# One state in eight with TensorE's product of dt*u and B, and background pieces, norms and tanh placed at other steps

## The chip, the cores and the metric

The kernel runs on one core of a Trainium2 chip. The core has five engines that work side by side and take their instructions in order: TensorE (PE, matrix products, with its weight loads PEld), VectorE (DVE), ScalarE (ACT), GpSimd (POOL) and SyncE (SP, which here issues most DMA transfers). Arrays lie in SBUF, 128 partitions wide; TensorE writes into PSUM, which has eight banks of 128 x 512 floats. The metric is the device time of one execution in microseconds (us).

## The reference

Sixteen sequences of 512 positions and 256 features pass through two layers, each with a residual and a layer norm. The first is a selective state-space model (forward, then a second one over its convolved output, backward), 512 channels wide with 16 states a channel; the second is a soft mixture of 16 experts with 64 slots each. Cut to what matters:

```python
xf, res = jnp.split(x @ in_proj_w.T, [D_INNER], axis=-1)
xf = silu(causal_dw_conv(xf, conv_w, conv_b))
y  = ssm(xf, res, ...)                        # forward
xb = silu(causal_dw_conv(xf, conv_b_w, conv_b_b))
y  = y + ssm(xb, res, ..., reverse=True)
x  = layernorm(x + y @ out_proj_w.T)
x  = layernorm(x + moe(x))                    # moe: see below

# in ssm: delta, B, C are projections of u (u = xf or xb)
dt = softplus(delta @ dt_proj_w.T + dt_proj_b)
dA   = einsum('bld,dn->bldn', dt, A)
dB_u = einsum('bld,bld,bln->bldn', dt, u, B)
dA_cum = exp(suffix_sum(dA))
xs = cumsum(dB_u * dA_cum, 1) / (dA_cum + 1e-12)
y  = einsum('bldn,bln->bld', xs, C) + u * D
y  = y * silu(res)

# in moe: x and the slot embeddings are normed
logits   = einsum('bnd,esd->bnes', x, se)
dispatch = softmax(logits, axis=1)            # over positions
combine  = softmax(logits over all slots)
slots = einsum('bnd,bnes->besd', x, dispatch)
eout  = (gelu(slots @ Wg + bg) * (slots @ Wu + bu)) @ Wd + bd
out   = einsum('bns,bso->bno', combine, eout)
```

All of it is in 32-bit floats.

## The kernel before

A tile has 128 channels as its partitions and the 512 positions along the free dimension; a direction has four such tiles (c = 0 to 3). The scan of a batch is four parts: forward and backward of tiles 0 and 1, then forward and backward of tiles 2 and 3 (`scan_part(b, r, p, ...)`, r the direction, p the pair of tiles). A part goes over the 16 states in eight pairs (n = 0, 2, ... 14) and the two tiles: 16 units a part, 64 a batch, 1,024 in all. A unit does, for two states of one tile:

- POOL, L356: `db = du * bs`, 128 x 1024, with du = dt*u of the tile (L304) and bs the two rows of B, spread over all partitions by a DMA (L352);
- ScalarE, for each state: `h = exp(A*dt)` into a PSUM bank of a ring of three (L361), and `th = tanh(...)` into SBUF (L363), which is the factor that the 1e-12 of the reference leaves;
- VectorE, for each state: the recurrence as one scan instruction, in place in PSUM (L365 forward, L367 backward), then `hg = (th + 1) * h` (L370);
- POOL, L371: `hg = hg * cs`, 128 x 1024, with cs the two rows of C;
- TensorE, L320: eight transposing products that add hg into an accumulator in PSUM (`add_up`, two units later).

db has three buffers, hg four, cs two, bs three.

Everything else is cut into pieces that are laid beside the units. A piece is what a generator does between two yields. `yield k` says that the next piece takes k PSUM banks of a ring of three (`bank`); `yield HOLD` says that TensorE's result is to be taken up at the next step. Three queues of the class `Side` hold the generators: `prep` (convolutions, projections, dt and rr of the parts to come; one piece at every unit), `front` (`finish`: output projection, norm and the dispatch of the batch before) and `back` (`experts` for two batches, then `combine` for each of the two). `front` and `back` are paced: a credit grows by the steps still to do over the units still to come, and a credit of one lets one piece go. `beside_scan` runs after every unit: it first takes up what is held in each queue, then lets each lay its piece. A queue that has just taken up a result may lay its next piece in the same step. A piece that takes banks goes only where the ring has room:

```python
oldest = min([x.hold for x in sides if x.hold is not None], default=count[0])
if count[0] - oldest + self.need > BANKS:
    break
```

At the end of a batch `front` is emptied, and `back` after every second batch. The tail, after the scan, has eight banks for the pieces: it empties what is left, with the last `finish`, and then does the last two batches' experts and combines.

Names that the change and the steps of the prediction touch: `scan_part` (L341) and its instructions above; `prep_pair` (L263), which makes dt, rr and du; `project_unit` (L240), which writes the rows of B and C to DRAM (bc); `Side.go`, `take_up`, `piece` (L391 to L422); `finish` (L503) with the norm (L533 to L549); `dispatch` (L567) with pl, et, pd, pq; `experts` (L627) with pg, pu, peo; `weights` (L761) with cl, cm, ctp; `combine` (L811) with cpo, its loads of the experts' results (ceo) and its norm (L857 to L860, scaled at L497). In `combine` a column of ones beside the experts' results gives the softmax's sum as column 257 of cpo, and VectorE inverts it (L853).

A scheduler orders the instructions of each engine; where the code says `late`, an instruction keeps its place in the program's order.

## Time and profile before

| | us |
|---|---|
| median of 3 runs | 5471.18 (5466.05 to 5471.56) |
| the profiled execution | 5474.83 |
| its span, first to last instruction | 5473.0 |
| db (L356), 1,024 instructions on POOL | 2424.6 |
| hg*cs (L371), 1,024 instructions on POOL | 2422.2 |
| scans (L365 and L367), 2,048 on VectorE | 2447.8 |
| (th+1)*h (L370), 2,048 on VectorE | 1349.1 |
| exp and tanh (L361, L363), 4,096 on ScalarE | 2854.7 |
| transposing products (L320), 8,192 on TensorE | 1219.4 |

The profile names an instruction by its line, engine, operation and tile. "Busy" is the time in which an engine executed; "idle before" is the time that it stood before instructions of a group, with what ended it. TensorE's clock is granted by a throttle; the profile gives the granted share. The scan ends some 278 us before the span does. The prediction shows the lines that it rests on.

### The profile page before, as it was taken

How to read it: one execution, taken by the hardware profiler on the slowest of the kernel's cores; microseconds unless marked ns; L12 is line 12 of the kernel's file. 1: busy time of each engine (PE TensorE's matmuls, PEld its weight loads, DVE VectorE, ACT ScalarE, POOL GpSimd, SP SyncE). 2: the span in 40 equal slices, each digit the busy share in tenths (PEclk: the TensorE clock that was granted, in tenths of full speed). 3: DMA queues.
4: the chain of work that ended last, by engine and by line, in shares of the span. 5: the costliest groups of instructions: out<-in, count | busy, mean ns of one | idle time of the engine just before them, and what ended most of it. 6: DMA issues, size and time to landing. Idle time of an engine off the chain costs nothing.

```text
span 5473.0 us, 67758 instructions
## 1 busy us (share of the span) xinstructions
PE 4001.2 (73%) x21317; PEld 3106.7 (57%) x21330; DVE 4522.5 (83%) x6212; ACT 4101.0 (75%) x6665; POOL 5003.5 (91%) x2547
## 2 busy tenths in 40 slices
PE   4556656677787777777777777877777776778887
PEld 2434444565555665566556655555655665567656
DVE  6787878889898888888888898989888888888722
ACT  6667777778778777878777887787778787778641
POOL 6999999999999999999999999999999999989700
PEclk7567777888998998889899888988988898999999
DMA  4333333465546664366544655455544666457435
GB/s 131 112 112 123 122 118 121 157 206 186 166 137 193 198 191 150 131 205 208 177 138 157 204 186 170 136 193 193 192 149 136 200 203 189 139 168 250 135 104 174
DMA packets 493949, 897.77 MB, mean 164 GB/s; under 512 B 44403, under 2 KB 291827, under 8 KB 493589
## 3 DMA queue, kind: packets, MB, share of 16 engines
q1 hardware_dynamic: 454836, 851.48, 48.4%
q10 hardware_dynamic: 38752, 41.95, 2.2%
q8 instruction: 169, 2.77, 0.2%
q14 instruction: 192, 1.56, 0.1%
HBM read 832.47 MB, written 60.82 MB: 163 GB/s over the span
## 4 chain that ended last, share of the span: by engine, by line
DVE 33%; ACT 24%; PE 19%; issue 11%; POOL 10%; DMA 3%; SPq 0%; DVEq 0%; ACTq 0%; POOLq 0%
DVE h L367 9%; DVE h L365 8%; DVE hg L370 8%; ACT h L361 5%; ACT th L363 5%; POOL db L356 4%; POOL hg L371 4%; PE acc L320 3%; PE px L247 2%; PE pg L718 2%; DVE rr L302 2%; PE cl L770 2%; ACT L361 2%; PE peo L703 2%; ACT ht L740 1%
## 5 line engine op out<-in xcount | busy, mean ns | idle before, releaser
L356 POOL TENSOR_TENSOR db<-du,bs 128x1024 f32<-128x1024 f32 x1024 | 2424.6, 2368 | 118.9 <-DVE h L365 50.5
L371 POOL TENSOR_TENSOR hg<-hg,cs 128x1024 f32<-128x1024 f32 x1024 | 2422.2, 2365 | 26.2 <-DVE hg L370 17.6
L370 DVE SCALAR_TENSOR_TENSOR hg<-th,h 128x512 f32<-128x512 f32 x2048 | 1349.1, 678 | 253.4 <-ACT th L363 139.7
L320 PE MATMUL acc<-ident,hg 128*128 128x128 f32 x8192 | 1219.4, 302 | 383.9 <-POOL hg L371 312.9
L320 PEld LDWEIGHTS acc<-ident,hg 128*128 128x128 f32 x8192 | 1074.4, 158 | 622.3 <-POOL hg L371 402.3
L367 DVE TENSOR_TENSOR_SCAN h<-h,db 128x512 f32<-128x512 f32 x1024 | 1226.2, 1219 | 191.5 <-ACT h L361 148.3
L365 DVE TENSOR_TENSOR_SCAN h<-h,db 128x512 f32<-128x512 f32 x1024 | 1221.6, 1219 | 181.9 <-ACT h L361 134.1
L361 ACT ACTIVATE h<-dt,A_f 128x512 f32<-128x512 f32 x1024 | 700.0, 684 | 316.6 <-DVE hg L370 313.8
L361 ACT ACTIVATE h<-dt,A_b 128x512 f32<-128x512 f32 x1024 | 699.8, 683 | 297.6 <-DVE hg L370 296.1
L363 ACT ACTIVATE th<-rr,Ah_b 128x512 f32<-128x512 f32 x1024 | 728.0, 711 | 0.3
L363 ACT ACTIVATE th<-rr,Ah_f 128x512 f32<-128x512 f32 x1024 | 726.9, 710 | 0.2
L703 PE MATMUL peo<-Wd,ht 128*128 128x256 f32 x1024 | 321.0, 469 | 196.2 <-DVE ht L687 136.0
L703 PEld LDWEIGHTS peo<-Wd,ht 128*128 128x128 f32 x1024 | 227.4, 232 | 269.7 <-DVE ht L687 143.0
L718 PE MATMUL pg<-st,Wg 128*128 128x128 f32 x2048 | 280.1, 300 | 77.4 <-ACT xb L222 39.7
L770 PE MATMUL cl<-seT,cx 128*128 128x512 f32 x512 | 275.7, 681 | 74.0 <-DVE rr L302 35.7
L718 PEld LDWEIGHTS pg<-st,Wg 128*128 128x128 f32 x2048 | 270.5, 215 | 87.5 <-ACT xb L222 41.2
L675 PE MATMUL pu<-st,Wu 128*128 128x128 f32 x2048 | 268.7, 287 | 30.4 <-ACT ht L740 11.8
L675 PEld LDWEIGHTS pu<-st,Wu 128*128 128x128 f32 x2048 | 256.5, 202 | 52.5 <-ACT ht L740 13.2
L574 PE MATMUL pl<-x2T,seT 128*128 128x512 f32 x512 | 260.0, 632 | 24.3 <-DVE xf L171 14.6
L606 PE MATMUL pq<-dis,xn 128*128 128x256 f32 x1024 | 254.6, 406 | 15.4 <-ACT dis L596 12.7
L844 PE MATMUL cpo<-ceo,ct 128*128 128x257 f32 x1024 | 244.1, 393 | 25.5 <-ACT ct L799 16.4
L606 PEld LDWEIGHTS pq<-dis,xn 128*128 128x128 f32 x1024 | 206.3, 207 | 49.8 <-ACT dis L596 15.6
(147 smaller groups left out, 5149.9 us busy)
## 6 DMA issues: line engine op xcount, KB each, us to landing
bs<-bc SPq DMA_DIRECT2D x512, 512.0 KB, 4.6
cs<-bc SPq DMA_DIRECT2D x512, 512.0 KB, 3.7
Wg<-in_Wg_dram SPq DMA_DIRECT2D x128, 512.0 KB, 5.4
Wu<-in_Wu_dram SPq DMA_DIRECT2D x128, 512.0 KB, 5.8
Wd<-in_Wd_dram SPq DMA_DIRECT2D x128, 512.0 KB, 5.9
bd<-in_bd_dram SPq DMA_DIRECT2D x128, 128.0 KB, 4.7
s_dram<-sl ACTq DMA_DIRECT2D x64, 256.0 KB, 3.0
st<-s_dram SPq DMA_DIRECT2D x128, 128.0 KB, 4.5
```

The source lines that it names most:

```text
L320: ins = nc.tensor.matmul(accs[c][:, s], hc[:, j, s], ident, is_transpose=True, start=False, stop=(last and j == 1 and lc == NL - 1),)
L356: nc.gpsimd.tensor_tensor(db, du.unsqueeze(1).to_broadcast([P, 2, L]), bs, ALU.mult)
L361: nc.scalar.activation(h, dt, AF.Exp, scale=w["A"][:, c, s])
L363: nc.scalar.activation(th, rr, AF.Tanh, bias=LN_1E12 / 2, scale=w["Ah"][:, c, s])
L365: nc.vector.tensor_tensor_scan(h, h, db[:, j, :], 0.0, ALU.mult, ALU.add)
L367: nc.vector.tensor_tensor_scan(h[:, ::-1], h[:, ::-1], db[:, j, ::-1], 0.0, ALU.mult, ALU.add)
L370: nc.vector.scalar_tensor_tensor(hg[:, j, :], th, 1.0, h, ALU.add, ALU.mult)
L371: nc.gpsimd.tensor_tensor(hg, hg, cs, ALU.mult)
L606: nc.tensor.matmul(pq[:, k * 256 : (k + 1) * 256], xn[:, lc, k * P : (k + 1) * P], dis[:, lc, :], start=(lc == 0), stop=(lc == NL - 1),)
L675: nc.tensor.matmul(pu[:, fc * P : (fc + 1) * P], got["Wu", e][:, k, fc * P : (fc + 1) * P], st[:, k, :, j * SL : (j + 1) * SL], start=(k = ...
L703: nc.tensor.matmul(po[:, :DM], ht[:, fc, :], got["Wd", e][:, fc, :], start=(fc == 0), stop=(fc == NF - 1))
L718: nc.tensor.matmul(pg[:, fc * P : (fc + 1) * P], got["Wg", e][:, k, fc * P : (fc + 1) * P], st[:, k, :, j * SL : (j + 1) * SL], start=(k = ...
```

## The change

1. States 5 and 13 of the 16 (`DIAG`) no longer get their product dt*u*B from POOL. In the pairs n = 4 and 12, POOL's db and the load bs have one state (k = 1). For the other, TensorE multiplies the transposed du (duT) by a diagonal matrix of B's row, 128 positions at a time, into a PSUM bank of the pieces' ring (`by_diagonal`), one unit ahead. The decay exp(A*dt) of that state goes to SBUF (dec), and VectorE scans with dec and the bank. The diagonals lie in DRAM, zeroed once; `project_unit` writes B's rows into them as single floats with a stride of 129, by a DMA of ScalarE's queue, and SP loads each as a 128 x 512 tile (dg) one pair of states ahead. duT is made at the start of each part (`turn_pair`: eight transposes, two copies by ScalarE).
2. A yield of GAP + k marks a piece that needs what was just taken up: it isn't laid in the step in which its queue took something up (except in the last batch, `hurry`). A yield of WAIT ends the queue's work for this step. Norms are scaled two such steps after their statistics.
3. tanh is issued one state ahead of exp; th has four buffers.
4. `combine` sums the softmax by ScalarE's accumulator at the exp, instead of a column of ones; et, yt, sl and others share one tag of two buffers (fr), and the experts' results the ring of weights (W). `back` is no longer emptied after every second batch.

The diff, cut to its core:

```diff
+DIAG = (5, 13)
+DIAG_SIZE = P * (P + 1)
...
-HOLD = -1
+HOLD, WAIT, GAP = -1, -2, 8
...
                 late(nc.scalar.activation(xf, xf, AF.Silu))
+                yield WAIT
                 yield from project_unit(b, 0, out)
...
             nc.sync.dma_start(bc[1], xd[XC:XW, :])
+            step = DIAG[1] - DIAG[0]
+            nc.scalar.dma_start(
+                diag_dram[r].rearrange("i l (p s) -> i l p s", p=P)[:, :, :, 0],
+                xd[XB + DIAG[0] : XB + NS : step, :].rearrange("i (l p) -> i l p", p=P),
+            )
...
+        def turn_pair(b, r, p, v):
+            yield 2
+            pts = []
+            for c in (2 * p, 2 * p + 1):
+                pt = bank(f"pdu_{b}_{r}_{c}")
+                for lc in range(NL):
+                    s = slice(lc * P, (lc + 1) * P)
+                    nc.tensor.transpose(pt[:, s], v[c][2][:, s], ident)
+                pts.append((c, pt))
+            yield HOLD
+            for c, pt in pts:
+                duT = p4.tile([P, L], F32, tag="duT", name=f"duT_{b}_{r}_{c}", bufs=2)
+                late(nc.scalar.copy(duT, pt))
+                v[c].append(duT)
...
             prep.drain()
-            prep.gens += [[1, g] for g in then]
+            prep.gens += [[1, g] for g in [turn_pair(b, r, p, v)] + then]
+            def by_diagonal(n, c):
+                diags.append(count[0])
+                made[n, c] = h = bank(f"hd_{b}_{r}_{n}_{c}")
+                for lc in range(NL):
+                    s = slice(lc * P, (lc + 1) * P)
+                    ins = nc.tensor.matmul(h[:, s], v[c][3][:, s], dg[:, s], start=True, stop=True)
...
+            gates = [tanh(*units.pop(0))]
             for n in range(0, NS, 2):
+                k = 1 if n + 1 in DIAG else 2
...
+                if n + 3 in DIAG:
+                    dg = p4.tile([P, L], F32, tag="dg", name=f"dg_{q}", bufs=1)
+                    nc.sync.dma_start(
+                        dg.rearrange("p (l s) -> p l s", l=NL),
+                        diag_dram[r, DIAG.index(n + 3), :, : P * P].rearrange("l (p s) -> p l s", p=P),
+                    )
...
-                    nc.gpsimd.tensor_tensor(db, du.unsqueeze(1).to_broadcast([P, 2, L]), bs, ALU.mult)
+                    nc.gpsimd.tensor_tensor(
+                        db[:, :k, :], du.unsqueeze(1).to_broadcast([P, k, L]), bs[:, :k, :], ALU.mult
+                    )
...
+                        if j < k:
+                            dec = h = ps_h.tile([P, L], F32, tag="h", name=f"h_{q}_{c}_{j}")
+                            hs[j] = (h, dec, db[:, j, :])
+                        else:
+                            h = made.pop((n + j, c))
+                            dec = p4.tile([P, L], F32, tag="dec", name=f"dec_{q}_{c}", bufs=2)
+                            hs[j] = (h, dec, h)
+                    for j in range(2) if k == 2 else (1, 0):
+                        nc.scalar.activation(hs[j][1], dt, AF.Exp, scale=w["A"][:, c, n + j : n + j + 1])
+                        if units:
+                            gates.append(tanh(*units.pop(0)))
...
-                            nc.vector.tensor_tensor_scan(h, h, db[:, j, :], 0.0, ALU.mult, ALU.add)
+                            nc.vector.tensor_tensor_scan(h, dec, add, 0.0, ALU.mult, ALU.add)
...
+                    nxt_n = n if c == chunks[0] else n + 2
+                    if nxt_n + 1 in DIAG:
+                        for x in sides:
+                            x.take_up()
+                        by_diagonal(nxt_n + 1, chunks[1] if c == chunks[0] else chunks[0])
                     beside_scan()
+                    if k == 1:
+                        diags.pop(0)
                     add_up(2)
...
             def take_up(self):
-                if self.hold is not None:
+                self.took = self.hold is not None or self.wait
+                if self.took:
                     self.go()
...
-                while self.gens and self.hold is None:
-                    oldest = min([x.hold for x in sides if x.hold is not None], default=count[0])
+                while self.gens and self.hold is None and not self.wait:
+                    if self.gap and self.took and gaps:
+                        break
+                    oldest = min([x.hold for x in sides if x.hold is not None] + diags[:1], default=count[0])
...
-            yield 0
+            yield WAIT
+            yield WAIT
             scaled(xt, xt, sh, rs)
...
-                yield 1
+                yield GAP + 1
                 pt = bank(f"pd_{i}")
...
-            for cm, cl in zip(cms, cls):
-                nc.scalar.activation(cm, cl, AF.Exp, bias=nm[:, 2:3])
-            yield 2
+            sm = p3.tile([P, 3], F32, tag="csm", name=f"csm_{i}", bufs=2 * NL)
+            for h, (cm, cl) in enumerate(zip(cms, cls)):
+                nc.scalar.activation(cm, cl, AF.Exp, bias=nm[:, 2:3], accum_out=sm[:, h : h + 1])
+            yield GAP + 2
...
             if kept is None:
                 stats = norm(0, NL)
-                yield 0
+                yield WAIT
+                yield WAIT
                 put(0, NL, *stats)
...
             front.drain()
-            if b % 2 == 0:
-                back.drain()
```

## The prediction

> **What bounds the kernel now.** First the busy shares and the slices of the page:
>
> ```profile
> PE 4001.2 (73%) x21317; PEld 3106.7 (57%) x21330; DVE 4522.5 (83%) x6212; ACT 4101.0 (75%) x6665; POOL 5003.5 (91%) x2547
> ...
> POOL 6999999999999999999999999999999999989700
> ```
>
> POOL is full until the scan ends and has nothing to do in the last two slices, so the run is a scan that POOL seems to pace (48 to 5195 us; L881 closes a batch, and its times give 323 us for batch 0, 317 to 324 for 1 to 14, 343 for 15) and a tail. Second, busy time by stage (columns: length, then PE, PEld, DVE, ACT, POOL busy, granted clock, DMA share, GB/s): batch 0, the heavy batches 3 to 14, roughly the last batch, and the two parts of the tail.
>
> ```profile
> 48.00:371.00 323.00, 165.11 (x724) 126.50 (x726) 267.17 (x310) 216.95 (x328) 319.10 (x151) 0.61 0.34 117
> 960.00:4800.00 3840.00, 2902.69 (x15862) 2267.55 (x15875) 3361.42 (x4603) 3055.08 (x4965) 3738.98 (x1878) 0.89 0.54 175
> 4800.00:5195.00 395.00, 320.97 (x1894) 263.43 (x1893) 323.65 (x483) 297.73 (x505) 347.83 (x174) 0.94 0.59 186
> 5195.00:5289.00 94.00, 76.37 (x285) 48.84 (x283) 20.93 (x51) 38.06 (x72) 4.96 (x12) 0.93 0.27 87
> 5289.00:5473.00 184.00, 148.78 (x861) 126.25 (x860) 42.20 (x128) 43.64 (x103) 9.71 (x32) 0.93 0.56 168
> ```
>
> Batch 0 carries little beside the scan (TensorE 51% busy), a heavy batch much (76%), and both take some 320 us: POOL is the bound in both, 319 of 323 us and 3739/12 = 311.6 of 320. But in a heavy batch VectorE is at 3361/12 = 280.1 us, and what it waits for comes third (waits of DVE, 960 to 4800 us):
>
> ```profile
> DVE h L365 <- ACT h L361: 117.3, 76, 4.8
> DVE hg L370 <- ACT th L363: 101.9, 51, 5.6
> DVE h L367 <- ACT h L361: 93.8, 79, 4.6
> DVE hg L370 <- PE acc L320: 35.2, 46, 2.1
> ```
>
> These and the smaller entries are about 427 us, 35.6 a batch, nearly all on ScalarE. With 4.3 us of gaps too small to be listed VectorE's own loop fills its 320 us. POOL's queue has been hiding that; take POOL's work away and VectorE is next. Fourth, where ScalarE comes late (timeline):
>
> ```profile
> 2169.70 0.69 ACT L361 ACTIVATE h<-dt,A_f 128x512 f32<-128x512 f32 x1 [1.85 <-DVE hg L370]
> ...
> 2175.74 2.08 ACT L497 ACTIVATE cx<-cx,c_sh,c_rs 128x256 f32<-128x256 f32 x4 [5.35 <-POOL c_sh L492]
> 2177.72 0.71 ACT L363 ACTIVATE th<-rr,Ah_f 128x512 f32<-128x512 f32 x1
> ...
> 2178.46 0.69 DVE L370 SCALAR_TENSOR_TENSOR hg<-th,h 128x512 f32<-128x512 f32 x1 [5.30 <-ACT th L363]
> ```
>
> The norm's scaling waits 5.35 us for statistics that stand behind two full-size products in POOL's queue; the tanh behind it is late, and VectorE stands for 5.30 us.
>
> **The change, part by part.** Prices, as total busy and mean ns:
>
> ```profile
> L356 POOL TENSOR_TENSOR db<-du,bs 128x1024 f32<-128x1024 f32 x1024 | 2424.6, 2368 | 118.9 <-DVE h L365 50.5
> L304 POOL TENSOR_TENSOR du<-dt,xf 128x512 f32<-128x512 f32 x64 | 80.0, 1272 | 9.7 <-ACT dt L285 9.5 <-ACT dt L289 0.2
> L333 PE MATMUL acc<-diagD_f,xf 128*128 128x128 f32 x512 | 77.8, 302 | 0.0
> L512 PE MATMUL pyt<-ident,res 128*128 128x128 f32 x256 | 40.3, 281 | 0.0
> ```
>
> *Removed.* Two states of sixteen lose their POOL product: 16 batches x 4 parts x 2 pairs x 2 tiles = 256 of 1,024 db shrink from 1024 to 512 columns. A 512-column product is 1.27 us (L304), so 2.37 - 1.27 = 1.09 us each, 279 us in all, 17.4 a batch. Exact halving would give 303; I take the row. The column of ones, its memsets (14 x 0.125 us) and 64 reciprocals go; sums, 128 accumulator reads (0.19 us each, as at L585) and small operations on VectorE come: under 2 us a batch.
>
> *Added on TensorE.* 1,024 products with a diagonal. L333 in both directions is 512 such products in the program, 1,024 instructions and 149 us here, so two instructions of 0.1455 us each: 298 us, 1.16 per unit. Turning du: 512 transposes at 40.3/256 = 0.157, 81 us. Together 379 us, 23.7 a batch; a heavy batch goes from 242 to some 261 of TensorE after what leaves for the tail (below). What hides it is TensorE's free quarter, at about 85% of 310 us no wide cover: the last stage of the scan ran at 81% and its batch took 343 us.
>
> *Added on ScalarE.* Eight copies a batch at 0.577 us (L517) = 4.6 us, accumulator reads 1.5; the 256 decays written to SBUF cost 27 ns more each (711 against 684, th and h). It had 255 of 320 us; 261 remain under 310. The first copy of du is due four units into a part; before it the part's pieces only wait.
>
> *Waits.* VectorE's second scan of a unit now waits for TensorE's product. Behind that wait stand the unit's second h*(th+1), then POOL's hg, then the next transposes. The product is issued one unit earlier, right behind the transposes of the unit four back; these end about when db of its own unit does, and the other state's 1.9 us (1.22 + 0.68) go first on VectorE. No row shows this wait: its ends are 0 and, were TensorE to begin only when VectorE asks, transposes (8 x 0.149) and product, 2.35 us x 16 = 38 us a batch. I take 2 us a batch: nearest is the 35.2 us in 12 batches that VectorE waits for acc, 2.9 a batch. Other end, a gain: these decays need no h buffer, 1/8 of the 211 us of waits on exp, 2.2 a batch. I let the two cancel.
>
> *Moved.* Norms two steps behind: in 1602 to 2244 us four such stalls (4.29, 3.40, 5.30, 1.85) cost VectorE 14.8 us in two batches, 7.4 a batch, gone if POOL answers within two units (9 us; it took 5 to 6.5). Tanh one ahead: the other tanh waits are (101.9 - 82)/12 < 2 a batch; I count 1. TensorE's pieces a step behind: TensorE waited 120 + 116 + 114 us on et, ht and cm in the heavy stage; that is TensorE's cover, worth nothing by itself.
>
> *DMA.* SP's queue gets 128 loads of a 256 KB diagonal, and the bs of 128 steps shrinks by 256 KB: bytes equal. The load stands ahead of cs and is issued units before its use; a load like it landed in 4.5 us (st). ScalarE's queue gets 32 writes of 1,024 single floats; a column load of 512 floats (D_f, 2 KB) landed in 2.3 us, so some 5 us, at least four units (18 us) ahead of the read. Without that cover: 32 x 5 = 160 us.
>
> The Trainium skill, "DMA: Bandwidth & Descriptors" (Latency and other measured facts), speaks against such writes: below 512 bytes a transfer is done by read-modify-write, off line rate. No row shows that price; by the rule they land later than my 5 us, which changes the sum only once the 18 us are used up, and then by up to the 160 us named.
>
> *The tail.* A piece that needs a copy just taken up now starts a step later, and the product holds one or two of the three PSUM banks in 6 of 16 steps. Followed through the queues, the background falls behind: when the scan ends, before leaves 5 of 13 steps of one combine; after leaves 10 of 40 expert steps and two whole combines. In instructions behind the last acc that is 64 pg, 80 pu, 40 peo, 48 cl, 48 ctp and 96 cpo more; at the tail's own busy time per instruction (0.128, 0.124, 0.274, 0.456, 0.154, 0.231) 80.6 us. The first part of the tail had 94 - 76.4 = 17.6 us of TensorE idle, which can hide some 10: +70.
>
> *The sum.* Batches 0 to 2, bound by POOL: 3 x 17.4 = -52. Heavy: POOL would allow 320 - 17.4 = 302.6; VectorE's loop 320 - 7.4 - 1 - 3 (waits that POOL's side caused) + 1 = 309.6. The later decides: 10.4 x 12 = -125. Batch 15 has fewer background steps (44 for 61): -12. Tail +70. Total -119. The profiled execution was 5474.8 us (5473.0 span), 0.07% over the median of 5471.2: 5471 - 119 = 5352, say 5355.
>
> **Rivals.** (a) *POOL stays the bound everywhere*: -279, -5 more as batch 15 has fewer background steps, +67 for the tail: 5471 - 217 = 5254. For it: light and heavy batches take the same time, so VectorE's waits looked free. Against: only 10 of 320 us separate its loop from POOL. Chance 0.17. (b) *The bound passes to VectorE and ScalarE at once*, as their waits do not shrink: heavy batches 316 to 320: 5430 to 5476. For it: 211 of 427 us are waits on exp, which the change hardly touches. Chance 0.16, 0.05 of it within 0.2%. (c) *Slower: TensorE's product comes late.* TensorE at 85% with in-order waits and one or two banks fewer; every unit of the two states holds VectorE for the product's own 1.16 us. Then 309.6 + 16 x 1.16 = 328 a heavy batch, 12 x 18.6 = +223: 5578. It decides from (5482 - 5355)/(12 x 16) = 0.66 us a unit. For it: the 343 us batch; against: a unit of lead. Chance 0.21. That the change does not do what it says is small: in its program 256 db have 512 columns.
>
> **How the numbers follow.** Forecast 0.46, around 5355 (5300 to 5420). Faster 0.46 + 0.17 + 0.11 = 0.74, within 0.2% 0.05, slower 0.21; 0.2% is what a measurement of this kernel can tell. The range, 5240 to 5510, takes in (a), (b) and the near half of (c).
>
> **What would show it.** Right: db x256 at 1.27 us and POOL near 4,720 us; no wait of cx or x on sh in the scan; heavy batches of 306 to 313 us; a tail of 348 us after the last L881 for 278. Wrong: waits of DVE on hd over 0.7 us a unit; POOL idle over 25 us a heavy batch; TensorE without the 379 us; a tail that did not grow.

## The result, and the profile after

The changed kernel takes 5470.31 us (median of 12 runs, 5459.48 to 5473.61), the kernel before, on the same chip, 5469.6 us (12 runs, 5460.49 to 5473.56): ratio 1.000 (95% interval 0.9991 to 1.0009). No change can be told. The profiled execution spans 5468.7 us, 4.3 us less than before's 5473.0.

Behind the zero stand moves of tens of microseconds. A batch ends with VectorE's last product of res and acc (L881 before, L987 after); by the times at which these start:

| stage | before, us | after, us | change | predicted |
|---|---|---|---|---|
| batches 0 to 2 (to the end of batch 2) | 1006.98 | 950.25 | -57 | -52 |
| heavy batches 3 to 14 | 3844.8 | 3870.5 | +26 | -125 |
| batch 15 | 343.3 | 317.1 | -26 | -12 |
| tail, behind the last such line | 277.9 | 330.9 | +53 | +70 |
| span | 5473.0 | 5468.7 | -4 | -119 |

The light batches, the last one and the tail went roughly where the prediction put them. The heavy ones did not: 323.2 us each (mean of 4 to 14) for 320.4 before and 309.6 predicted. First the page of the kernel after: busy time with its share of the span and the count, and POOL in 40 slices.

```profile
PE 4239.6 (78%) x23889; PEld 3381.1 (62%) x23890; DVE 4512.5 (83%) x6275; ACT 4164.7 (76%) x6906; POOL 4733.4 (87%) x2537
...
POOL 6999999999989989998998989999999989998400
```

POOL has lost 270 us, as meant (5003.5 before), and its row of nines has gaps: it now waits. Busy time by stage of the kernel after (length, then PE, PEld, DVE, ACT, POOL busy, granted clock, DMA share, GB/s): batch 0, batches 4 to 14, batch 15, and the two parts of the tail.

```profile
48.00:355.00 307.00, 179.12 (x882) 139.14 (x884) 262.30 (x305) 224.82 (x342) 299.90 (x150) 0.70 0.39 126
1266.00:4821.00 3555.00, 2824.44 (x16184) 2260.44 (x16185) 3083.60 (x4268) 2850.49 (x4715) 3248.96 (x1714) 0.90 0.54 171
4821.00:5138.00 317.00, 263.01 (x1597) 218.34 (x1595) 263.26 (x380) 246.92 (x421) 277.34 (x146) 0.90 0.59 186
5138.00:5232.00 94.00, 84.18 (x428) 63.27 (x428) 26.77 (x76) 35.40 (x79) 3.28 (x8) 1.00 0.58 179
5232.00:5469.00 237.00, 206.66 (x1092) 163.32 (x1092) 62.01 (x184) 72.48 (x175) 13.11 (x40) 0.97 0.47 144
```

In batch 0 POOL is busy 300 of 307 us: there it still paces, and the batch ends 12.5 us sooner (batches 1 and 2 are 22 us shorter each). In a heavy batch it is busy 3249/11 = 295.4 of 323.2 us and idles 28: it has stopped being the bound, and the batch did not get shorter. No engine is full there: VectorE 280.3, TensorE 256.8, ScalarE 259.1. So the time is in what they wait for. Waits of VectorE, 960 to 4800 us, in the kernel after (total, times, longest):

```profile
DVE h L442 <- ACT h L433: 187.4, 89, 9.9
DVE h L440 <- ACT h L433: 69.9, 43, 5.5
DVE ht L784 <- PE pu L772: 60.3, 25, 9.1
DVE hd L442 <- PE hd L388: 34.8, 25, 3.9
DVE xf L182 <- ACT xf L176: 28.7, 11, 5.0
DVE hg L445 <- PE acc L354: 26.5, 26, 4.6
```

The 101.9 us of waits on tanh (hg <- th) are gone from the head of the list, but the waits on exp have grown from 211 to 257 us, and new ones on TensorE have come: pu, the product hd, and xf. One of the stalls on exp, in the timeline of ScalarE in the kernel after (start, us, what):

```profile
3229.57 1.28 ACT L240 ACT_TABLE_LOAD   x1
3230.86 1.92 ACT L240 ACTIVATE xb<-xb 128x2048 f32<-128x2048 f32 x1
3232.69 0.56 ACT L612 COPY yt<-pyt 128x512 f32<-128x512 f32 x1
3233.27 1.28 ACT L834 ACT_TABLE_LOAD   x1
3234.56 0.37 ACT L834 ACTIVATE ht<-pg,bg_cols 128x128 f32<-128x128 f32 x1
3234.83 1.91 ACT L837 ACTIVATE ht<-pg,bg_cols 128x128 f32<-128x128 f32 x7
3236.75 1.28 ACT L433 ACT_TABLE_LOAD   x1
3238.04 0.69 ACT L433 ACTIVATE h<-dt,A_f 128x512 f32<-128x512 f32 x1
```

and in VectorE's (in brackets the idle time before it and who ended it):

```profile
3238.84 1.23 DVE L440 TENSOR_TENSOR_SCAN h<-h,db 128x512 f32<-128x512 f32 x1 [5.18 <-ACT h L433]
```

No norm is in it. A silu and a GELU of the background fall together; each has its own function, so ScalarE loads function tables three times (3.84 us) beside 4.8 us of work, and VectorE stands 5.18 us for the next exp. The prices of the change's parts came out as costed: the small product on POOL, TensorE's product (2 instructions each) and the turning of du (total, mean ns, then idle time ahead of it and its releasers):

```profile
L419 POOL TENSOR_TENSOR db<-du,bs 128x512 f32<-128x512 f32 x256 | 326.8, 1277 | 107.6 <-issue 42.0 <-DVE h L442 35.5 <-DVE h L440 22.2
L388 PE MATMUL hd<-dg,duT 128*128 128x128 f32 x2048 | 303.2, 296 | 104.6 <-DVE rr L320 29.1 <-ACT th L397 18.5 <-issue 16.2
L333 PE MATMUL pdu<-ident,du 128*128 128x128 f32 x512 | 82.2, 307 | 20.6 <-ACT et L682 8.5 <-ACT yt L612 5.2 <-POOL du L322 2.6
```

So it is not one of these prices that was off. What a heavy batch does with 17 us of POOL's time given back is the question of the experiments.

### The profile page after: what moved, and what is told of

Read it like the earlier page. It is cut to its first block, busy times and chain, and to the rows that moved or that the text cites. A ratio compares the mean times of both kernels' runs of the same rounds, so it can differ in the third digit from the quotient of the medians.

```text
span 5468.7 us, 73513 instructions
## 1 busy us (share of the span) xinstructions
PE 4239.6 (78%) x23889; PEld 3381.1 (62%) x23890; DVE 4512.5 (83%) x6275; ACT 4164.7 (76%) x6906; POOL 4733.4 (87%) x2537
## 4 chain that ended last, share of the span: by engine, by line
DVE 39%; PE 20%; ACT 19%; issue 12%; POOL 5%; DMA 2%; DVEq 0%; SPq 0%; ACTq 0%; POOLq 0%
DVE h L440 10%; DVE hg L445 9%; DVE h L442 9%; ACT h L433 4%; ACT th L397 4%; PE acc L354 3%; PE pu L772 2%; POOL hg L446 2%; DVE hd L440 2%; POOL db L419 2%; PE cpo L946 2%; DVE hd L442 2%; DVE rr L320 2%; ACT L433 1%; PE cl L867 1%
## 5 line engine op out<-in xcount | busy, mean ns | idle before, releaser
L419 POOL TENSOR_TENSOR db<-du,bs 128x1024 f32<-128x1024 f32 (+1 forms) x1024 | 2140.9, 2093 | 288.7 <-issue 104.5
L442 DVE TENSOR_TENSOR_SCAN h<-h,db 128x512 f32<-128x512 f32 x896 | 1074.2, 1219 | 261.7 <-ACT h L433 250.6
L445 DVE SCALAR_TENSOR_TENSOR hg<-th,h 128x512 f32<-128x512 f32 x1792 | 1188.0, 679 | 66.2 <-PE acc L354 29.4
L440 DVE TENSOR_TENSOR_SCAN h<-h,db 128x512 f32<-128x512 f32 x896 | 1072.6, 1219 | 99.7 <-ACT h L433 92.8
L433 ACT ACTIVATE h<-dt,A_b 128x512 f32<-128x512 f32 x896 | 607.6, 680 | 104.1 <-DVE hg L445 102.8
L433 ACT ACTIVATE h<-dt,A_f 128x512 f32<-128x512 f32 x896 | 608.5, 681 | 99.0 <-DVE hg L445 97.0
L772 PE MATMUL pu<-st,Wu 128*128 128x128 f32 x2048 | 309.2, 315 | 138.8 <-issue 38.1
L772 PEld LDWEIGHTS pu<-st,Wu 128*128 128x128 f32 x2048 | 293.3, 227 | 176.5 <-issue 55.9
L388 PE MATMUL hd<-dg,duT 128*128 128x128 f32 x2048 | 303.2, 296 | 104.6 <-DVE rr L320 29.1
L388 PEld LDWEIGHTS hd<-dg,duT 128*128 128x128 f32 x2048 | 275.6, 209 | 116.1 <-DVE rr L320 25.5
L946 PE MATMUL cpo<-ceo,ct 128*128 128x256 f32 x1024 | 249.0, 400 | 44.0 <-ACT x2T L657 26.6
```

The lines of the kernel that those rows point to most:

```text
L388: ins = nc.tensor.matmul(h[:, s], v[c][3][:, s], dg[:, s], start=True, stop=True)
L419: nc.gpsimd.tensor_tensor(db[:, :k, :], du.unsqueeze(1).to_broadcast([P, k, L]), bs[:, :k, :], ALU.mult)
L433: nc.scalar.activation(hs[j][1], dt, AF.Exp, scale=w["A"][:, c, n + j : n + j + 1])
L440: nc.vector.tensor_tensor_scan(h, dec, add, 0.0, ALU.mult, ALU.add)
L442: nc.vector.tensor_tensor_scan(h[:, ::-1], dec[:, ::-1], add[:, ::-1], 0.0, ALU.mult, ALU.add)
L445: nc.vector.scalar_tensor_tensor(hg[:, j, :], th, 1.0, h, ALU.add, ALU.mult)
```

## The experiments

Each is given with its median, its ratio to the kernel before on the same chip, and from its profiled run the mean light batch (1, 2), heavy batch (4 to 14) and tail. e1, e2, e8, e9, e13, e14, e15 and e17 leave out the product of states 5 and 13 (their scan takes that of states 4 and 12), and e3 computes other functions; before, after, e4 to e7, e10, e12 and e16 do the whole computation. In the edits shown, `...` marks what is left out.

| run | us | ratio (95%) | light | heavy | tail |
|---|---|---|---|---|---|
| before (profiled run) | | 1 | 317.9 | 320.4 | 277.9 |
| after (profiled run) | 5470 | 1.000 (0.9991 to 1.0009) | 295.9 | 323.2 | 330.9 |
| e1_pool_only | 5376 | 0.983 (0.9813 to 0.9843) | 303.4 | 315.9 | 278.2 |
| e2_no_products | 5336 | 0.975 (0.9740 to 0.9769) | 295.0 | 318.3 | 254.8 |
| e3_one_table | 5252 | 0.960 (0.9585 to 0.9617) | 292.9 | 307.9 | 324.2 |
| e4_placement_only | 5411 | 0.989 (0.9878 to 0.9907) | 310.9 | 319.9 | 261.7 |
| e5_h_ring | 5513 | 1.007 (1.0055 to 1.0085) | 296.4 | 329.5 | 264.1 |
| e6_no_gap | 5548 | 1.013 (1.0119 to 1.0149) | 296.0 | 331.9 | 302.0 |
| e7_light_only | 5375 | 0.981 (0.9800 to 0.9829) | 296.8 | 319.5 | 261.9 |
| e8_norm_only | 5451 | 0.996 (0.9947 to 0.9972) | 298.7 | 323.2 | 282.2 |
| e12_light_old_norm | 5466 | 1.000 (0.9989 to 1.0008) | 299.8 | 325.6 | 267.7 |
| e13_no_products_old_norm | 5455 | 0.997 (0.9962 to 0.9982) | 298.1 | 324.5 | 264.5 |
| e14_tanh_only | 5371 | 0.981 (0.9798 to 0.9828) | 304.9 | 315.6 | 274.8 |
| e15_no_tanh | 5315 | 0.971 (0.9697 to 0.9726) | 294.4 | 315.9 | 260.6 |
| e16_light_no_tanh | 5361 | 0.980 (0.9781 to 0.9810) | 296.4 | 318.9 | 260.5 |
| e17_no_products_no_gap | 5392 | 0.985 (0.9836 to 0.9869) | 298.2 | 320.9 | 260.0 |

### POOL's saving, TensorE's work, ScalarE's functions, the order of pieces

The first theory was that ScalarE's bursts bound a heavy batch once POOL does not; the rival, that TensorE's added work does. e1 is the kernel before with POOL's saving alone:

```
+                k = 1 if n in (4, 12) else 2
...
-    nc.gpsimd.tensor_tensor(db, du.unsqueeze(1).to_broadcast([P, 2, L]), bs, ALU.mult)
+    nc.gpsimd.tensor_tensor(db[:, :k, :], du.unsqueeze(1).to_broadcast([P, k, L]), bs[:, :k, :], ALU.mult)
...
-    nc.vector.tensor_tensor_scan(h, h, db[:, j, :], 0.0, ...)
+    nc.vector.tensor_tensor_scan(h, h, db[:, j % k, :], 0.0, ...)
```

> The kernel before with POOL's db of states 5 and 13 left out (the scan of these states takes the db of states 4 and 12, so the output is not the reference's); no product on TensorE, no other edit. If ScalarE's bursts pace VectorE in the heavy batches (3 to 14), these stay at 314 to 320 us while batches 0 to 2 fall by 17 to 22 us each: total 5350 to 5420. If TensorE's new work is what ate the gain, nothing stands in the way here and every batch falls by some 17 us: total 5190 to 5230.

e2 is the kernel after without by_diagonal, turn_pair, the diagonals and their DMAs (db[:, j % k, :] as in e1):

```
-    prep.gens += [[1, g] for g in [turn_pair(b, r, p, v)] + then]
+    prep.gens += [[1, g] for g in then]
...
-    by_diagonal(nxt_n + 1, chunks[1] if c == chunks[0] else chunks[0])
```

> The changed kernel without TensorE's products, the turned du, the diagonals and their DMAs, db still halved (states 5 and 13 scan with the db of 4 and 12; the output is not the reference's): the new placement of pieces, norms and tanh with POOL's saving free of charge. If TensorE's 379 us and the held PSUM banks are the cause, heavy batches fall from 322 to 303 to 306 us: total 5240 to 5290. If ScalarE's bursts are, they stay at 314 to 321: total 5400 to 5470.

e3 is the kernel after with three functions put in place of others, so that no table is loaded between them:

```
-AF.Silu, AF.Gelu, AF.Softplus
+AF.Tanh, AF.Tanh, AF.Exp
```

> The changed kernel with silu and gelu computed as tanh and softplus as exp, so that ScalarE never changes its function table (345 loads of 1.28 us gone, 440 us of ScalarE; the output is not the reference's). If ScalarE's bursts pace the heavy batches, these fall from 322 to 304 to 310 us: total 5270 to 5340. If TensorE does, they stay within 4 us of 322: total over 5410.

e4 is the kernel after with all sixteen states on POOL (e2 with k = 2 throughout):

```
-                k = 1 if n + 1 in DIAG else 2
+                k = 2
```

> The changed kernel with all 16 states on POOL again: only the placement (pieces a step behind, norms two steps, tanh one ahead, softmax sums) is new. POOL then paces every batch at 317 to 322 us in either theory; the tail grows by some 40 to 55 us as background work is left over: total 5500 to 5530. If the placement itself hurts VectorE's loop, heavy batches are over 324.

The saving alone (e1) is worth 14.5 us in a light batch and 4.5 in a heavy one, and 96 us in all: it agrees with ScalarE's theory (5350 to 5420) and not with TensorE's. In the new order (e4 against e2) it is worth 15.9 and 1.6. e3 agrees as strongly: without 329 of 330 table loads (423 us in the program, 26 a batch; the 345 that I had given are the kernel before's) heavy batches lose 15.3 us, the largest gain there of any run, though all of TensorE's products are there. Waits of VectorE in e3, batches 4 to 14 (the list of the kernel after above covers one batch more):

```profile
DVE h L442 <- ACT h L433: 102.5, 52, 7.0
DVE ht L784 <- PE pu L772: 42.2, 12, 7.0
DVE hg L445 <- PE acc L354: 27.4, 27, 3.5
DVE h L440 <- ACT h L433: 26.3, 20, 4.8
```

Waits on exp alone come to 128.8 us in 11 batches; with tanh they fall from 22.8 to 12.5 us a batch; ScalarE is 28 us a batch less busy (230.8 for 259.1), about what the loads took, for the functions put in take as long as those that they replace (the silu of L240 1912 ns, the tanh in its place 1911). But e2 fell between the theories (5336; 5400 to 5470 and 5240 to 5290 had been given): taking the products away helps after all, 4.9 us a heavy batch and 76 us of tail. And e4 missed what I gave it: 5411 for 5500 to 5530, its tail 262 us for a growth of 40 to 55. The new order does not lengthen the tail, it shortens it by 16 us; all of the growth in the kernel after is the products'. By stage, the new order alone (e4 against before) gains 17 us in batches 0 to 2, 10 in the heavy ones and 16 each in batch 15 and the tail; the products (e2 to the kernel after, with their turns and DMAs) cost 8, 55, -10 and 76 us there, 129 in all. That is what uses up the 134 us (2.5%) by which e2 is below the kernel before.

### What the products cost: time on TensorE or a bank held

e5 takes the product's bank from the decays' ring:

```
-                diags.append(count[0])
-                made[n, c] = h = bank(f"hd_{b}_{r}_{n}_{c}")
+                made[n, c] = h = ps_h.tile([P, L], F32, tag="h", name=f"hd_{b}_{r}_{n}_{c}")
...
-                        for x in sides:
-                            x.take_up()
...
-                    if k == 1:
-                        diags.pop(0)
```

> The kernel after with one thing changed: the product with the diagonal takes its PSUM bank from the ring of the decays h and not from the three banks that TensorE's background pieces share. TensorE issues exactly the same products at the same places; the whole computation is there. What is behind TensorE's lateness in the kernel after (VectorE's waits on pu, hd and xf, 11 us a heavy batch) and behind the tail that grew from 278 to 331 us? Theory 1, held banks: a product that holds one of three banks keeps background pieces from being issued, they pile up for the tail; then with the ring of h the tail goes back to 255 to 285 us, the pu and xf waits shrink below 3 us a batch, and the time is 5380 to 5430. Theory 2, TensorE's own 379 us: the products and turns delay the pieces whatever bank they use; then the tail stays at 310 to 335 us, the waits stay near 11 us a batch, and the time is within 25 us of the kernel after's 5470. A third possibility: two rings of h fewer for ScalarE's decays make exp later (waits of VectorE on h from ScalarE, 22 us a batch now, up to 30): 5450 to 5550 with a short tail.

The tail goes from 331 to 264 us, where theory 1 had it, with TensorE doing the same products: 67 of the 76 us by which the products lengthen it are the held bank, which keeps background pieces waiting until the scan has ended. The waits on pu and xf vanish too (0.3 and 0.2 us a batch for 4.7 and 2.2).

The edit takes one thing more along than its expectation says. Ahead of a product the kernel after takes up what is held, and `beside_scan` does so again in the same step. A queue that took something up the first time has `took` false after the second, so in these steps, four of a part's sixteen, a piece marked GAP may go at once and both WAITs of a norm pass in one step; there the rule of part 2 of the change does not hold. In e5 it does hold. That starts pieces later, and later starts lengthen the tail (e6, below, starts them earlier and has a tail 29 us shorter), so it can't be what shortened it. For the waits on pu and xf the bank and the double taking-up were not told apart.

The time is 5513, above theory 1's 5380 to 5430, since a new wait took their place. The range of the third possibility (5450 to 5550 with a short tail) holds it, but the wait is mostly on hd and not, as that said, on exp. Waits of VectorE in e5, batches 4 to 14:

```profile
DVE h L441 <- ACT h L432: 211.8, 91, 8.7
DVE hd L439 <- PE hd L387: 81.5, 37, 6.8
DVE h L439 <- ACT h L432: 54.7, 37, 2.3
DVE hd L441 <- PE hd L387: 37.2, 27, 2.7
DVE nm L671 <- PE pl L666: 36.0, 14, 4.5
```

hd costs 118.7/11 = 10.8 us a batch for 4.1, and exp 24.2 for 22.1. With three decays' banks shared among decays and products, a product has to wait until a bank of theirs is free; heavy batches are 329.5 us. Neither ring has a bank to spare. Whether TensorE's 24 us a batch would cost anything with a bank of its own for hd was not tried: the rings hold three, two and three banks, all eight that the tail's pieces have when the scan is over.

### The parts of the new order, one by one

e6 is the kernel after with the later start of TensorE's pieces left out; e17 is the same edit on e2:

```
-            prep.piece()
+            prep.piece(False)
-                x.paced_piece(gaps=not hurry)
+                x.paced_piece(gaps=False)
```

> The kernel after without the rule that a TensorE piece which needs a copy just taken up starts a step later; products, turns, placement and the norms' waiting stay; the whole computation is there. The background is then issued earlier and less is left at the end of the scan (1 expert step and two whole combines for 10 and two). If the rule is what shrank TensorE's in-order waits, heavy batches get longer by 3 to 8 us without it (more waits of VectorE on pu and xf) and the tail shorter by some 15 us: 5490 to 5550. If TensorE's waits are covered anyway and VectorE's loop is set by ScalarE's lateness, heavy batches stay within 1.5 us of 323 and only the tail gains: 5440 to 5475.

> The run without TensorE's products and turns (5335, heavy batches 318.3; two of POOL's sixteen products left out), without the rule that a piece of TensorE which needs a copy just taken up starts a step later: norms behind and tanh ahead stay. With the products that rule was worth 8.7 us a heavy batch. If it is worth that much here too, heavy batches go to 325 to 328 and the time to 5410 to 5460, and TensorE's in-order waits on copies (waits of VectorE on acc, cpo, peo) show it; if it served the products alone: 317 to 320 and 5310 to 5350.

e6, at 5548, is where its first theory had it: 331.9 us a heavy batch, 8.7 more, of which acc is the largest part (the wait of hg on acc is 7.7 us for 1.8; pu and xf, which the theory had named, fall), and a tail 29 us shorter. In e17 the rule is worth 2.6 us a heavy batch (320.9 for 318.3), between the two theories and nearer the second; 5392 us lies between their totals. Hg's wait on acc is again the largest growth (7.0 for 2.5). The prediction had counted these later starts as worth nothing by themselves.

e8 is e1 with the norms two steps behind and nothing else:

```
-            yield 0
+            yield WAIT
+            yield WAIT
             scaled(xt, xt, sh, rs)
```

> The run with POOL's two products of sixteen left out and nothing else (5376; states 5 and 13 take the products of states 4 and 12, nothing added on TensorE) with one more part of the change: norms scaled two steps behind. My prediction counted the stalls behind a norm's late statistics at 7.4 us a heavy batch, to be had once ScalarE no longer waits. If that step holds, heavy batches go from 315.9 to 307 to 310 us and the time to 5280 to 5310. If ScalarE's lateness only moves from the norms to its other bursts (function changes of the background's activations), as the run with the new order alone suggests, heavy batches stay at 313 to 317 and the time at 5345 to 5390.

It is 7.3 us a heavy batch *slower* than e1, outside both theories. VectorE's waits, batches 4 to 14, first in e1:

```profile
DVE h L368 <- ACT h L364: 101.2, 69, 4.8
DVE h L370 <- ACT h L364: 95.0, 69, 4.6
DVE hg L373 <- ACT th L366: 59.1, 47, 2.8
DVE hg L373 <- PE acc L320: 34.6, 46, 2.0
```

and then in e8:

```profile
DVE h L370 <- ACT h L364: 134.7, 62, 4.6
DVE h L368 <- ACT h L364: 94.4, 72, 3.6
DVE hg L373 <- PE acc L320: 66.7, 37, 3.8
DVE csm L859 <- PE cpo L850: 39.6, 18, 3.5
DVE hg L373 <- ACT th L366: 35.2, 44, 2.7
```

Less waiting on tanh (59 to 35), more on exp (196 to 229), and on TensorE (acc, cpo) over 70 us more. TensorE's own queue shows the latter (waits of PE in e8, 1300 to 4750 us):

```profile
PE pd L597 <- ACT et L593: 133.8, 40, 8.7
PE ctp L796 <- ACT cm L789: 97.7, 29, 8.2
PE ptx L199 <- ACT th L366: 65.9, 10, 7.5
```

The transposes ptx waited 14.9 us in e1, 2.5 at most; in e8 they stand at the head of TensorE's queue for up to 7.5 us, with the scan's sums behind them. So the waiting of norms by itself makes TensorE late. With the later start of pieces and the change's other buffers and sums (e15) the batch is back at 315.9, which is why the parts must be judged together; which of these makes up for it was not tried apart. Two runs take the norms' waiting back where the other parts are in place: e12 from e7 (below), e13 from e2.

> The run without TensorE's products and turns (5335, heavy batches 318.3; two of POOL's sixteen products left out, states 5 and 13 take those of states 4 and 12) with the norms scaled one step behind their statistics as in the kernel before; tanh one ahead and TensorE's later pieces stay. This isolates the waiting of the norms where POOL is not the bound: by my prediction's 7.4 us heavy batches go to 325 and the time to 5425; if the waiting is worth nothing, 317 to 320 and 5320 to 5350; if it costs, 311 to 316 and 5250 to 5310.

> The run with the products in batches 0 to 2 alone (5375, heavy batches 319.5, tail 262; the whole computation is there), with the norms scaled one step behind their statistics as in the kernel before. My prediction put the norms' stall at 7.4 us a heavy batch, gained by waiting two steps: by it this run is 7 us a heavy batch longer, 5450 to 5470. If the waiting is worth nothing (ScalarE's lateness only moves to its other bursts), it stays within 2 us a batch: 5355 to 5400. If the waiting itself costs, as it did without the other parts of the change, heavy batches are 3 to 7 us shorter: 5290 to 5340.

Here the waiting is worth 6.2 and 6.1 us a heavy batch (324.5 to 318.3, 325.6 to 319.5), near the predicted 7.4; e12 lies where my prediction's step put it, e13 30 us above (its profiled run was 18 us under its median). But the nearness is in good part luck, for what the step says is to go, ScalarE's wait for the statistics, hardly does. Waits of ScalarE, batches 4 to 14, before, then in e13 and in e2:

```profile
ACT x L497 <- POOL m_sh L492: 65.1, 11, 6.6
ACT cx L497 <- POOL c_sh L492: 58.5, 11, 5.7
ACT x L564 <- POOL m_sh L559: 46.0, 11, 5.6
ACT cx L564 <- POOL c_sh L559: 21.0, 6, 6.1
ACT x L564 <- POOL m_sh L559: 34.8, 11, 4.5
ACT cx L564 <- POOL c_sh L559: 21.7, 6, 4.3
```

That is 11.2 us a heavy batch before, 6.1 in e13 and 5.1 in e2: two steps instead of one take 1 us off it (2, with 14.9 us more in e13 that cx waits for another of POOL's tiles, rr) where the batch gains 6. VectorE's stalls on exp and tanh that overlap such a wait of ScalarE come to 6.6 us a heavy batch before, 2.7 in e13 and nil in e2, so less than half of the 6 us is the stall that I had named; where the rest comes from is open. And e1, with POOL's saving alone, has 7.8 us of the one and only 1.5 of the other: a less busy POOL had by itself taken most of the norms' stall. Yet VectorE's waits on exp and tanh there are 23.2 us a batch, for 25.0 before.

In all, the new order gives a heavy batch nothing once POOL is relieved (318.3 in e2 for 315.9 in e1). Does tanh's order eat it? e14 is e1 with tanh one state ahead (and the buffers of sl and yt made one ring, for room):

```
+            gates = [tanh(*units.pop(0))]
...
                         nc.scalar.activation(h, dt, AF.Exp, scale=w["A"][:, c, s])
-                        nc.scalar.activation(th, rr, AF.Tanh, bias=LN_1E12 / 2, scale=w["Ah"][:, c, s])
+                        if units:
+                            gates.append(tanh(*units.pop(0)))
+                        th = gates.pop(0)
```

> The run with POOL's two products of sixteen left out and nothing else (5376, heavy batches 315.9; states 5 and 13 take the products of states 4 and 12) with one more part of the change: the gate's tanh one state ahead of its decay (four buffers of th for three; to make room, the buffers of sl and yt become one ring of two). By my prediction it gives 1 us a heavy batch: 314 to 316, 5355 to 5380. If VectorE's waits on tanh only turn into waits on exp, within 2 us: 5355 to 5400. If tanh ahead is what costs 8.6 us in the run with old norms, heavy batches are 321 to 326: 5430 to 5490.

e15 is e2 with tanh behind its own exp:

```
-                        if units:
-                            gates.append(tanh(*units.pop(0)))
+                        gates[j] = tanh(n + j, c)
```

> The run without TensorE's products and turns (5335, heavy batches 318.3; two of POOL's sixteen products left out), with tanh back behind its own decay: norms two steps behind and TensorE's later pieces stay. If tanh ahead costs 8 us a heavy batch: 309 to 312, 5230 to 5280, and my prediction's 309.6 is what the rest of the change gives. If it is worth its 1 us: 318 to 321, 5335 to 5375. If it is what takes the waits on tanh away (5 to 8 us a heavy batch): 323 to 328, 5390 to 5460.

Tanh ahead alone changes nothing in a heavy batch (315.6 for 315.9), and taking it out of e2 gains 2.4 us. It does what it is for, the waits on tanh go (5.4 us a batch in e1, nil in e14), and exp takes them over (17.8 to 23.6). Both times lie outside the 8 us theory, and e15's outside its other two as well. Side by side, all with POOL's saving and without products, VectorE's waits on ScalarE's exp and tanh together, per heavy batch:

| norms behind | tanh ahead | later pieces* | heavy batch | exp + tanh |
|---|---|---|---|---|
| no | no | no (e1) | 315.9 | 23.2 |
| no | yes | no (e14) | 315.6 | 23.6 |
| yes | no | no (e8) | 323.2 | 24.0 |
| yes | yes | no (e17) | 320.9 | 22.5 |
| yes | no | yes (e15) | 315.9 | 22.2 |
| no | yes | yes (e13) | 324.5 | 27.5 |
| yes | yes | yes (e2) | 318.3 | 21.6 |

*e2, e13, e15 and e17 also have the change's other buffers and its sums in place of a column of ones.

No order gets below 315.6 us, and none gets the waits on exp and tanh below 21.6 (all the waits of e1, 30.1 us, with VectorE's 281.6 of work and 4.2 of small gaps make its 315.9). What is named tanh in one is named exp in the next. Only taking work from ScalarE lowered that sum (e3, to 12.5). Which part of e13 makes it 9 us longer than e14 (the later start with old norms, or the buffers) was not tried apart.

### Room for ScalarE to run ahead

If ScalarE's bursts bind, a deeper ring between it and VectorE should absorb them. e9 (from e2) and e10 (from e4):

```
-    dec = h = ps_h.tile([P, L], F32, tag="h", ...)
+    dec = h = (ps_h.tile([P, L], F32, tag="h", ...) if j == 0
+               else p4.tile([P, L], F32, tag="hS", ..., bufs=3))
-    th = p4.tile([P, L], F32, tag="th", ..., bufs=4)
+    th = p4.tile([P, L], F32, tag="th", ..., bufs=6)
```

> The kernel after without TensorE's products and turns (its run: 5335, heavy batches 318.3; POOL's two products of sixteen left out, states 5 and 13 take those of states 4 and 12), with more room for ScalarE to work ahead of VectorE: the second state of each pair keeps its decay in SBUF (three buffers) and the first in the three PSUM banks, and th has six buffers for four. Theory, short lead: a burst of ScalarE (a norm, a change of function, softplus) stalls VectorE because ScalarE is never more than three decays ahead of it; with twice the lead VectorE's waits on exp fall from 21.6 us a heavy batch to under 12 and heavy batches from 318 to 300 to 310: 5200 to 5270. Rival, no slack to build a lead: ScalarE with 256 us of work and as many of waiting on VectorE never gets ahead, or SBUF costs the scan more: heavy batches within 3 us of 318 or longer, 5310 to 5380.

> The run with the new order and all 16 states on POOL (5411, heavy batches 319.9, light ones 310.9; the whole computation is there) with the same deeper rings for decays and th. If the short lead holds VectorE, heavy batches fall to POOL's own work, 312 to 315 us, and light ones stay at 311: 5330 to 5365. If not, it stays at 5400 to 5430.

6850 and 7046 us, ratios 1.253 (1.2512 to 1.255) and 1.289. This missed by 1500 us and says nothing on the lead, for VectorE itself became the bound (94% busy). Its groups in e9; in e2 the first took 678 ns, the scans 1219:

```profile
L428 DVE SCALAR_TENSOR_TENSOR hg<-th,h 128x512 f32<-128x512 f32 x2048 | 2475.0, 1231 | 54.6 <-PE acc L344 29.0
L425 DVE TENSOR_TENSOR_SCAN h<-h,db 128x512 f32<-128x512 f32 x1024 | 1651.9, 1636 | 57.2 <-ACT h L416 49.2 <-issue 8.0
L423 DVE TENSOR_TENSOR_SCAN h<-h,db 128x512 f32<-128x512 f32 x1024 | 1629.3, 1621 | 4.6 <-POOL db L403 3.9 <-ACT h L416 0.7
```

With h in SBUF for one state in two, the same instructions take 82% and 34% longer on the mean. In this kernel h has to be in PSUM, and that is full; so a deeper lead stays untried.

### Products where they pay

e7 keeps TensorE's products for batches 0 to 2; e16 is e7 with tanh behind its own exp. Both do the whole computation.

```
+            DG = DIAG if b < 3 else ()
-                k = 1 if n + 1 in DIAG else 2
+                k = 1 if n + 1 in DG else 2
```

> The kernel after with the products of TensorE in batches 0 to 2 alone, where the background is light; from batch 3 on all 16 states are on POOL, as in the run with the new order alone; the whole computation is there. Theory: the saved POOL time is worth its full 15 us a batch only where VectorE does not wait for ScalarE, in the light batches, and in heavy ones it is worth some 4 and costs 11 in TensorE's lateness. Then batches 0 to 2 go from 311 (the new order alone) to 296, heavy batches stay at 320, the tail at 262: 5411 - 3 x 15 = 5366, range 5350 to 5385, faster than both kernels. If POOL's saving were worth something in the heavy batches too, by the order of pieces alone, this run would lose it: above 5411.

> The run with the products in batches 0 to 2 alone (5375, heavy batches 319.5; the whole computation is there), with tanh back behind its own decay. If tanh ahead costs: heavy batches at POOL's 312 to 315, 5290 to 5330, the fastest whole kernel here. If it is worth 1 us or nothing: 5365 to 5395. If it takes the waits on tanh away: 5430 to 5480.

e7 came where it was put: 5375 for 5366, light batches 296.8 for 296, heavy 319.5 for 320, tail 261.9 for 262. e16 has the lowest median of the whole kernels here, 5361 us, 2.0% below both (ratio 0.9781 to 0.9810). Against e7 that is 14 us, where its first theory had 60; the intervals of the two overlap and their heavy batches differ by 0.6 us, so no effect of tanh's order is shown.

## Why the prediction was wrong, point by point

It forecast 5355 us, a gain of 119; there is none. The time lies inside the range only because that held the rivals.

- **POOL's saving** (279 us, from the 512-column product's price) was right: 270 us, the product 1277 ns.
- **Batches 0 to 2, bound by POOL** (-52): -57, near by luck. POOL's saving alone gives -43 there (e1). The new order, which I had put at nothing in these batches, gives -17 (e4).
- **The step that failed: "VectorE's loop 320 - 7.4 - 1 - 3 + 1 = 309.6" in the heavy batches**, -125 in all for a measured +26. Its terms as the runs have them: POOL's side, -3, is -4.5 (e1). Norms and tanh, -8.4, are +2.4 together with the rest of the order (e1 to e2). The flaw is in subtracting: I took stalls off VectorE's loop by the name of what it waited for. POOL's saving alone took most of the norms' stall (6.6 us to 1.5), tanh ahead took all of the waits on tanh (5.4 us to nil, e14), and each time VectorE waited nearly as long on exp: 25.0 us a batch on exp and tanh before, 23.2 in e1, 23.6 in e14, 22.8 after. The timelines and e3 point to the function changes of ScalarE as what it is then late for; that the same lateness moves there, stall by stall, is not shown. Nor did the two steps do what I counted on: ScalarE's waits on late norms were to be gone and are half of before's.
- **The products' cover.** "TensorE's free quarter" hid the 379 us only in batches 1 and 2 (295.9 us for 295.0). The wait on hd I put at 2 us a batch, offset by fewer decays' waits; hd is 4.1, and I had no term for what stands behind the products in TensorE's queue or for their bank: pu 4.7 for 1.3, xf 2.2. By e2 to the kernel after that makes +4.9. So 320.4 - 4.5 + 2.4 + 4.9 = 323.2.
- **Later pieces "worth nothing by itself"**: wrong, 2.6 us a batch without products and 8.7 with them.
- **Batch 15** (-12): -26, of which the new order alone is -16 (e4). **The tail** (+70): +53, but of two parts, products +76 (e2 to after) and the order -16 to -23 (e4, e2). The sum came near by luck: for the order alone I had expected a longer tail.
- **The DMA** (nothing, or up to 160 us): nothing that shows. No wait of TensorE for the diagonals (dg) or their DMA stands in the trace of the kernel after; how long the single-float writes took to land it does not show. The line on transfers below 512 bytes that the prediction cites stands under "Specifications" of that page.
- **A reading**: "nearly all on ScalarE" was 336 of the 427 us; the rest was nearly all TensorE's and POOL's.
- **The rivals.** (b), the bound passing to VectorE and ScalarE at once (316 to 320, 5430 to 5476), is what happened to POOL's relief: e1 and e15 stand at 316. That 5470 lies in its range is luck, for the heavy batches are at 323.2, with the products' cost in them. It deserved more than 0.16: I had the 211 us of waits on exp in view and counted them as untouched, not as the place where the others would go. (c), the late product, had its mechanism but not its size: hd 4.1 us in 16 units is 0.26 us a unit, below the 0.66 from which it decides; pu and xf, which it lacked, went away in e5. (a) is excluded: POOL idles 28 us a heavy batch.
- **The signs I had named**: POOL idle over 25 us a heavy batch came true and meant what it said. ScalarE still waits for late norms, about half of before's:

```profile
ACT cx L592 <- POOL c_sh L587: 34.8, 10, 6.4
ACT x L592 <- POOL m_sh L587: 27.2, 11, 3.9
```

(Waits of ScalarE in the kernel after, 1300 to 4750 us; before's are shown beside e13.)

## What to carry to other kernels

A wait listed for an engine is not a sum to be taken off its loop: if its releaser has bursts of its own, the wait can come back under the next name, as it did here, so ask what that engine does when it is no longer late, and price only the work that leaves it. Moving work off the bound paid where that engine alone paced (here the light batches, 15 us each) and paid little, 4.5 of 17 us, where VectorE's own loop of work and waits stood close behind it; split such a change by stage, as e7 and e16 do. Work that takes a shared PSUM bank has to be costed by what then waits for the bank as well, here 67 us of tail, and not by its time on TensorE alone.

## What the hardware showed unasked

Two VectorE operands in SBUF beside a busy POOL are dear: from PSUM and SBUF the 128x512 gate took 678 ns (e2); in e9, with th and h both in SBUF for half of the instructions, the mean was 1231 ns, and POOL's 128x1024 product of hg went from 2367 to 2657 ns. Without POOL they are not: of the 1,024 gates in e9 with both in SBUF, the 23 that no instruction of POOL overlaps took 681 ns on the mean, the other 1,001 took 1818. The Trainium skill, "SBUF — State Buffer", says that a VectorE operation with two SBUF inputs and one of GpSimd exclude each other; the runs agree in kind. A change of ScalarE's function took 1.28 us in the timeline above, the next activation starting 1.29 us after the load began; the same skill's "ScalarE: Activation LUTs" (What ACT_TABLE_LOAD costs) gives 2.66 us with a drain, which these rows do not show.
